# Graph layer on one core: one unit of rows in 72 fetched by SyncE instead of gathered by GpSimd

## The chip, the cores and the metric

The kernel runs on one NeuronCore of a Trainium2 chip. A core has five engines that run side by side, each with its own instruction queue: TensorE (PE, matrix products; its weight loads are shown apart as PEld), VectorE (DVE), ScalarE (ACT), GpSimd (POOL) and SyncE (SP), which computes nothing and issues transfers. Transfers run on 16 DMA engines that all queues share. The metric is the device time of one execution in microseconds.

## The reference

One layer of a graph network over 50,000 nodes with 160 features each (64 scalars and 32 vectors of three) and 1,650,000 edges, which come sorted by target node `dst`. Each edge also has four numbers `e0, e1[3]`. Cut to what matters:

```python
ss, vv = s[src], v[src]                       # the rows of x, fetched by edge
dot  = einsum('eui,ei->eu', vv, e1)
out0 = C0 * (ss * e0 @ W1 + dot * INV3 @ W2)
p3 = (ss @ W3)[:, :, None] * e1[:, None, :] * INV3
p4 = einsum('eui,uw->ewi', vv * e0[:, :, None], W4) * INV3
p5 = einsum('eui,uw->ewi', cross(vv, e1), W5) * INV6
m  = concatenate([out0, C1 * (p3 + p4 + p5)])
m_agg = segment_sum(m, dst, num_segments=n)   # sum over the edges of a node
h  = m_agg times Ws and Wv                    # linear per node
y  = x + (x + relu(h));  return layernorm(y)
```

Everything is linear in the row `x[src]` and in the edge's four numbers. So it is enough to sum, per target node, the four products of an edge number with the 160 values of the source row, and to apply one combined weight of 4 x 160 by 160 afterwards.

## The kernel before

**Units, groups, pairs.** A *unit* is 128 edges, one per partition. Six units (`G`) make a *group*, whose targets lie within 32 consecutive nodes (`W`); two groups (`PG`) make a *pair*; 20 groups (`SG`) are loaded together. There are 2087 groups, 1044 pairs and 12,522 units. The main loop `for p, (s, g, ng) in enumerate(pairs)` does, for each pair:

- `gather` (L314 to L322): one indirect DMA per unit on GpSimd (L319) that fetches 128 rows of `x`, 640 bytes each, into one slot of the tile `xg`. That tile has four buffers, so GpSimd can be up to four pairs ahead.
- `spread` (L324 to L334): VectorE makes `hot` (which of the 32 nodes each edge belongs to, L328) and `ha` (`hot` times the four edge numbers, L331).
- `group_sums` (L336 to L350): TensorE multiplies `ha` with the rows (L343), six units accumulate into one PSUM tile `ps`, and VectorE transposes it into `sums` (L349). The first matmul of a pair waits until the gathers of the whole pair have landed.
- `fetch(p)`: described below; with `HELP` empty it does nothing.

Every two pairs the weights are applied to four groups (`phc`, L579), and every block of 128 nodes is put together from these (`phb`, L639), normalised (`norm1` to `norm3`, the last writing `o` at L199) and sent out (`out<-o`, L735).

**Self edges.** Each node's edge to itself is not gathered. For the part of the list behind the first 100 groups, `pack` removes these edges from the rows of the list on VectorE and stores the shortened rows to DRAM one partition at a time (`edges<-prow`, `selves<-mine`, both L563, with the addresses loaded into registers at L546). `load` (L254) reads them back as `r`. The self edges' part is computed from `xt` and `sa` (L592, L596) in `own` (L615 to L629).

**Order.** SyncE's instructions run in the order in which the program writes them (`tc.manual_schedule(engines={ET.SP})`): in each pair a load if it is due, then `fetch(p)`, the stores of `pack`, `xt` and `sa` of a block seven pairs ahead, and the sends of finished blocks, each written eight pairs after the block's last group. The other engines' instructions are ordered by a planner when the program is built. All gathers stand in order on GpSimd, which has little else to do.

**The helper that is built in.** `HELP` names engines and periods. Where it is filled, the code before the main loop picks one unit in so many and a pair `q` that uses it, always the last unit of that pair, and divides its 128 rows into batches, spread over the pairs before (L646 to L661):

```python
nbatch = P // ROWS[eng]                     # ROWS = {ET.SP: 32, ET.Activation: 16}
at = [int(first + i * period / nbatch) // (PG * G) for i in range(nbatch)]
q = at[-1] + 2
```

`fetch(p)` (L665 to L678) then issues batch `i` at pair `p`: it loads 32 addresses into registers and starts 32 transfers of one row each:

```python
_, at = nc.values_load_multi_w_load_instructions(
    offsets[s][u:u + 1, i * nr:(i + 1) * nr], engines=[eng], ...)
for j, v in enumerate(at):
    r = i * nr + j
    queues[eng].dma_start(xr[r:r + 1, :].bitcast(U8),
                          xbytes[ds(v, 4 * D)].rearrange("(o f) -> o f", o=1))
```

The addresses come from `cast` (L265 to L276), which, when `HELP` is not empty, multiplies the source indices of each load by 640 on ScalarE into `offsets[s]`. The tile `xr` has three buffers.

Of the kernel before, what the change touches and what calls it, by code (L numbers as in the profile page):

```python
# [45 lines left out]
ET = mybir.EngineType  # L46
# [20 lines left out]
PG = 2  # L67
SG = 20

HELP = {}  # L70
HEAD = 100
RP = 128
RS = 16
# [30 lines left out]
def tile_gnn_resnorm(ctx: ExitStack, tc: tile.TileContext, x, src, dst, attr, W1, W2, W3, W4, W5, Ws, Wv, out, n_edges):  # L104
# [120 lines left out]
    with tc.tile_pool(name="once", bufs=1) as once, tc.tile_pool(name="raw", bufs=2) as rawp, \  # L225
# [18 lines left out]
        offsets = {}  # L244
        evict = nc.vector.tensor_copy if ET.Activation in HELP else nc.scalar.copy

# [18 lines left out]
        def cast(loaded):  # L265
            s, n, ri, sf, df, af = loaded
            if ri is not None:
                rf = rawp.tile([P, 2, P], F32, name="rf")
                begun.append(nc.scalar.copy(rf[:n], ri[:n]))
                sf, df = rf[:n, 0, :], rf[:n, 1, :]  # L270
            if HELP:

# [374 lines left out]
        batches, helped = {}, {}  # L647
        for h, (eng, period) in enumerate(HELP.items()):
            first = PG * G + h * period // 2
# [359 lines left out]
```

## Time and profile before

| | |
|---|---|
| median of the timed runs | 15705.15 us (15704.62 to 15706.36, 3 runs) |
| the profiled execution | 15737.51 us, span of its instructions 15735.7 us |
| GpSimd busy | 11891.8 us, 76% |
| TensorE matmuls busy | 8152.5 us, 52% |
| VectorE busy | 6035.6 us, 38% |
| ScalarE busy | 499.5 us, 3% |
| bytes moved | 1215.93 MB, 77 GB/s on average |

Times in the profile are in us unless marked ns. "Busy" leaves out register, branch, semaphore and DMA-issuing instructions, so SyncE has no busy row; its instructions are seen in the timeline as SPq. In a line of the costliest groups stand the code line, engine, operation, written tile and read tiles, shapes, count, then the busy time, the mean of one in ns, the idle time before them, and what ended that idle time. "issue" means that the engine waited for nothing that the profile shows. A line of the waits reads: who waited, for whom, the total, how often, the longest.

### The profile page before, as it was taken

Reading aid. Unit: us, or ns where it says so; the run is one execution under the profiler, and the core shown is the slowest. Engines: PE = TensorE matmul, PEld = TensorE weight load, DVE = VectorE, ACT = ScalarE, POOL = GpSimd, SP = SyncE. Lnnn points to the kernel's source line nnn. Section 1 sums busy time; section 2 is a strip of 40 time slices with the busy share of each in tenths; the row PEclk is TensorE's granted clock in tenths of the full one; section 3 lists DMA queues with packets and bytes.
Section 4 is the critical chain, followed back from the end, with each engine's and each line's share of the span. In section 5 each row is a group of like instructions: output and inputs, shape, how many; then the busy total and the mean of one; then the engine's idle time right before and its main releaser. Section 6 shows DMA issues by size and latency. Waiting matters only on the chain. (4 is left out here: it accounts for less than half of the span.)

```text
span 15735.7 us, 122013 instructions
## 1 busy us (share of the span) xinstructions
PE 8152.5 (52%) x38505; PEld 7452.0 (47%) x38506; DVE 6035.6 (38%) x11070; ACT 499.5 (3%) x1392; POOL 11891.8 (76%) x12536
## 2 busy tenths in 40 slices
PE   4554545555455555555455554554545555455555
PEld 4444545444454444444444444454444444444444
DVE  5342524325253342533425343352433425234222
ACT  0000000000000000000000000000000000000000
POOL 7777777777777777777777777777777777777777
PEclk7777777777777777777777776777777777777777
DMA  3323333233233323333233332332333332332232
GB/s 79 84 74 84 75 76 80 74 82 75 76 80 77 80 75 76 80 78 79 73 79 78 77 81 74 83 75 75 80 76 81 75 82 73 76 79 73 73 75 68
DMA packets 806901, 1215.93 MB, mean 77 GB/s; under 512 B 280851, under 2 KB 585160, under 8 KB 802278
## 3 DMA queue, kind: packets, MB, share of 16 engines
q0 software_dynamic: 601056, 1026.60, 26.6%
q1 hardware_dynamic: 203770, 180.19, 3.9%
q8 instruction: 323, 5.29, 0.1%
q14 instruction: 312, 2.56, 0.1%
q10 hardware_dynamic: 1440, 1.29, 0.0%
HBM read 1135.77 MB, written 71.40 MB: 77 GB/s over the span
## 5 line engine op out<-in xcount | busy, mean ns | idle before, releaser
L319 POOL DMA_INDIRECT xg<-in_x,si x12522 | 11887.6, 949 | 3825.5 <-issue 3777.2
L343 PE MATMUL ps<-xg,ha 128*128 128x160 f32 x25044 | 5686.4, 408 | 7298.0 <-DMA xg<-in_x,si 5676.0
L343 PEld LDWEIGHTS ps<-xg,ha 128*128 128x128 f32 x25044 | 5451.3, 281 | 7580.6 <-issue 6593.5
L349 DVE STREAM_TRANSPOSE sums<-ps 128x320 f32<-128x320 f32 x1044 | 530.7, 512 | 6311.9 <-PE ps L343 6240.0
L331 DVE TENSOR_TENSOR ha<-hot,pk 128x1536 f32<-128x1536 f32 x1044 | 1802.6, 1730 | 206.3 <-PE ps L343 206.3
L627 DVE TENSOR_SCALAR t<-yx,sa 128x160 f32<-128x160 f32 x391 | 147.5, 377 | 2585.8 <-PE yx L623 2585.5
L623 PE MATMUL yx<-BWh,xT 80*128 80x320 f32 x3128 | 1032.0, 472 | 156.6 <-ACT xT L617 152.7
L579 PE MATMUL phc<-BWk,sums 128*128 128x160 f32 x5220 | 820.6, 305 | 22.2 <-DVE t L629 19.7
L623 PEld LDWEIGHTS yx<-BWh,xT 80*128 80x128 f32 x3128 | 599.3, 202 | 439.2 <-ACT xT L617 237.4
L579 PEld LDWEIGHTS phc<-BWk,sums 128*128 128x128 f32 x5220 | 750.7, 193 | 49.6 <-issue 40.3
L639 PE MATMUL phb<-hp,hot 128*128 128x160 f32 x3474 | 562.0, 307 | 6.1 <-DVE t L629 4.3
L328 DVE TENSOR_TENSOR hot<-bank,rel 128x384 f32<-128x384 f32 x1044 | 551.1, 540 | 0.1
L639 PEld LDWEIGHTS phb<-hp,hot 128*128 128x128 f32 x3474 | 503.1, 194 | 60.5 <-issue 50.4
L629 DVE SCALAR_TENSOR_TENSOR t<-yx,sa,t 128x160 f32<-128x160 f32 x1173 | 442.6, 377 | 82.4 <-PE yx L623 67.8
L511 DVE COPY_PREDICATED prow<-marks,prow 128x2370 f32<-128x2370 int32 (+8 forms) x160 | 442.5, 2765 | 0.0
L617 ACT COPY xT<-ptx 80x256 f32<-80x256 f32 x391 | 143.8, 368 | 8133.7 <-PE ptx L615 8133.3
L581 ACT COPY hp<-phc 128x160 f32<-128x160 f32 x522 | 150.3, 288 | 5316.5 <-PE phc L579 5284.5
L511 DVE COPY_PREDICATED pra<-marks,pra 128x1580 f32<-128x1580 int32 (+8 forms) x160 | 304.5, 1903 | 0.0
L605 DVE TENSOR_TENSOR hot<-bank,rr 128x512 f32<-128x512 f32 (+2 forms) x391 | 285.3, 730 | 0.0
L640 DVE TENSOR_TENSOR phb<-phb,t 128x160 f32<-128x160 f32 x391 | 127.4, 326 | 136.1 <-PE phb L639 134.4
L615 PE MATMUL ptx<-ident,xt 128*80 128x128 f32 (+1 forms) x782 | 154.5, 278 | 38.4 <-ACT hp L581 34.1
L193 ACT ACTIVATE rstd<-mv,eps_t 128x1 f32<-128x1 f32 x391 | 115.2, 295 | 1707.3 <-DVE mv L188 1630.5
(144 smaller groups left out, 2600.6 us busy)
## 6 DMA issues: line engine op xcount, KB each, us to landing
xg<-in_x,si POOLq DMA_INDIRECT x12522
edges<-prow SPq DMA_DIRECT2D x1994, 18.5 KB
r<-edges SPq DMA_DIRECT2D x99, 360.0 KB
selves<-mine SPq DMA_DIRECT2D x1992, 0.5 KB
xt<-in_x SPq DMA_DIRECT2D x390, 80.0 KB
out<-o SPq DMA_DIRECT2D x390, 80.0 KB
pra<-in_attr SPq DMA_DIRECT2D x15, 1580.0 KB
sa<-selves SPq DMA_DIRECT2D x390, 2.0 KB
```

The source lines that it names most:

```text
L319: got.append(nc.gpsimd.indirect_dma_start(out=xg[:, j, :], out_offset=None, in_=x, in_offset=bass.IndirectOffsetOnAxis(ap=placed[0][:, u + ...
L328: nc.vector.tensor_tensor(hot[:, :n], slotsP[:, 0:W].unsqueeze(1).to_broadcast([P, n, W]), rel[:, u:u + n].unsqueeze(2).to_broadcast([P, n ...
L331: nc.vector.tensor_tensor(ha[:, :n], hot[:, :n].unsqueeze(2).to_broadcast([P, n, NK, W]), pk[:, :, u:u + n].rearrange("p k u -> p u k").un ...
L343: mm = nc.tensor.matmul(ps[:, j // G, :], ha[:, j].rearrange("p k w -> p (k w)"), xr, start=j % G == 0, stop=j % G == G - 1)
L349: nc.vector.transpose(at[:, :, i:i + ng, :].rearrange("p b g w -> p g b w"), ps[:, :ng].rearrange("p g (b f) -> p g b f", f=FB))
L511: nc.vector.copy_predicated(what[:n, a:e], mi[:, r].unsqueeze(2).to_broadcast([n, e - a, what.shape[2]]), what[:n, a + d:e + d])
L579: nc.tensor.matmul(ph[:ng * W], at[:, b, :ng].rearrange("p g w -> p (g w)"), BWk[:, b, :], start=b == 0, stop=b == ND - 1)
L605: nc.vector.tensor_tensor(hot2[:, :len(cs)], slotsP.unsqueeze(1).to_broadcast([P, len(cs), P]), rr[:, :len(cs)].unsqueeze(2).to_broadcast( ...
L615: nc.tensor.transpose(pt[:, i, :nb], xt[:nb, i * H:(i + 1) * H], ident[:nb, :nb])
L623: nc.tensor.matmul(y[:nb], xT[:, i, :nb], BWh[:, i, ks, :], start=i == 0, stop=i == 1)
L629: nc.vector.scalar_tensor_tensor(t[:nb], y[:nb, i], sa[:nb, k:k + 1], t[:nb], op0=ALU.mult, op1=ALU.add)
L639: nc.tensor.matmul(ph[:nb], hot2[:r, i, :nb], hp[:r], start=i == 0, stop=i == len(cs) - 1)
```

## The change

One constant is filled. SyncE becomes a helper with a period of 72 units.

```diff
-HELP = {}
+HELP = {ET.SP: 72}
```

With it, one unit in 72 is left out of the gathers (`n - len(others)` in `gather`), its rows come from `xr`, `fetch` issues the batches on SyncE, and `cast` makes the addresses on ScalarE. Each batch holds 32 rows, so a unit has four, and its pair is the second one after the pair of its last batch. Nothing else in the source differs; the planner orders the other engines anew.

## Prediction

> **What bounds the kernel now.** I read the page's busy shares first, then the costliest groups, then the timeline of an ordinary stretch, and last the queue of SyncE.
>
> ```profile
> span 15735.7 us, 122013 instructions
> PE 8152.5 (52%) x38505; PEld 7452.0 (47%) x38506; DVE 6035.6 (38%) x11070; ACT 499.5 (3%) x1392; POOL 11891.8 (76%) x12536
> L319 POOL DMA_INDIRECT xg<-in_x,si x12522 | 11887.6, 949 | 3825.5 <-issue 3777.2
> L343 PE MATMUL ps<-xg,ha 128*128 128x160 f32 x25044 | 5686.4, 408 | 7298.0 <-DMA xg<-in_x,si 5676.0
> q0 software_dynamic: 601056, 1026.60, 26.6%
> ```
>
> GpSimd looks 76% busy, but nearly all its idle time is "issue": it waits for nothing and is simply between two gathers. Busy plus idle is 11887.6 + 3825.5 = 15713.1 us, over 12522 gathers 1.2548 us each. That is the whole span except 9.8 us before the first gather and 18.7 us after the last. TensorE's largest idle share, 5676.0 us, is waiting for gathered rows. The DMA engines are far from full: the gather queue takes 26.6% of them.
>
> The timeline, columns start, duration, engine, line, operation, shows the pace, and what SyncE does beside it:
>
> ```profile
> 5063.20 0.30 SPq L563 DMA_DIRECT2D edges<-prow  x1
> 5063.60 0.27 SPq L563 DMA_DIRECT2D selves<-mine  x1
> 5063.96 0.23 SPq L563 DMA_DIRECT2D edges<-prow  x1
> 5064.29 0.23 SPq L563 DMA_DIRECT2D selves<-mine  x1
> 5064.61 0.23 SPq L563 DMA_DIRECT2D edges<-prow  x1
> ...
> 5189.08 0.48 DVE L199 TENSOR_SCALAR o<-y,mv,rstd 128x160 f32<-128x160 f32 x1
> 5189.59 0.37 SPq L735 DMA_DIRECT2D out<-o  x1
> 5189.81 0.95 POOL L319 DMA_INDIRECT xg<-in_x,si  x1 [0.30 <-issue]
> 5190.01 0.42 SPq L254 DMA_DIRECT2D r<-edges  x1
> 5191.06 0.95 POOL L319 DMA_INDIRECT xg<-in_x,si  x1 [0.30 <-issue]
> 5192.31 0.95 POOL L319 DMA_INDIRECT xg<-in_x,si  x1 [0.31 <-issue]
> ...
> 5197.88 6.17 PE L343 MATMUL ps<-xg,ha 128*128 128x160 f32 x24 [10.51 <-DMA xg<-in_x,si]
> ```
>
> Two things are to be seen. GpSimd keeps 1.25 us a gather while SyncE issues one-row transfers: the pace does not yield to SyncE's traffic. And SyncE's one-row transfers, with the register move before each, start 0.32 us apart. The matmul group shown is that of pair 343 (12 gathers, 24 matmuls a pair), ready 2 to 3 us after its last gather, and done within about 6 us of the pair's 12 x 1.2548 = 15.06.
>
> SyncE's own waits and the register loads (duration is least/median/most):
>
> ```profile
> SPq L735 <- DVE o L199: 10633.5, 284, 133.6
> SPq L563 <- DMA edges<-prow: 161.8, 360, 1.2
> L546 SPq TENSOR_LOAD <-spots x272: 1143/1206/1472, 293.5 to 14869.2; - x136
> L563 SPq DMA_DIRECT2D selves<-mine x2117: 227/228/1027, 364.8 to 14873.9; - x193
> ```
>
> SyncE is idle two thirds of the span, nearly all of it held at the send of a finished block until VectorE has made `o`.
>
> **The change part by part.**
>
> *Removed from GpSimd.* The helper starts at unit 12 and takes one unit every 72, as long as the pair that uses it is before pair 1044: 173 units (pairs 7, 13, 19, ... 1039). 173 x 1.2548 = **217 us** off the queue that sets the end. Against the profiled execution: 15735.7 - 217 = 15519. That execution is 0.2% above the median of the timed runs; the same 217 us there gives 15705 - 217 = 15488.
>
> [...]
>
> *Added to SyncE's queue.* Each unit is 128 rows in 4 batches of 32. A batch is a load of 32 addresses into registers, nearest row L546 with 1.206 us for 16 addresses, so 2.41 us, and 32 times a move and a one-row DMA, nearest row `selves<-mine` (one partition, 512 B, dynamic address), 0.322 us apart, so 10.3 us: 12.7 us. In all 173 x 4 x 12.7 = 8.8 ms on an engine that now uses 4236 one-row stores x 0.41 (mean spacing in their bursts, small waits included) + 272 x 1.206 + 391 blocks x 1.33 for three transfers + about 80 for the loads = 2.66 ms, or 15.3 us for every 72 units. The period for 72 units becomes 71 x 1.2548 = 89.1 us; SyncE needs 4 x 12.7 + 15.3 = 66.1 of it, 74%. It fits.
>
> The spacing of a row fetch itself is not in the trace: it reads HBM and writes SBUF, where the stores do the reverse. Bounds: below, 0.32, since the sequencer's part is the same; above, the stores' mean of 0.41, stretched because each SyncE transfer waits for the one eight before it (the 360 short waits shown) and the 18.5 KB `edges` rows hold one DMA engine for 0.71 us each. A fetched row has 640 B, and the packets of `xt<-in_x`, also HBM to SBUF, are all in within about 1 to 1.5 us of issue, under 8 x 0.32 = 2.6. I take 0.32; at 0.41 SyncE needs 77.4 of 89.1 us, which still fits.
>
> [...]
>
> *The wait that is added.* The last unit's two matmuls of a helped pair wait for SyncE's rows, and everything behind them on TensorE with them. The batches stand in SyncE's written order six, five, three and two pairs ahead, and SyncE is often held at a send. Worst place seen: the send of pair 339, shown above, is released at 5189.6, 47 us after that pair's matmuls. Behind it stand two batches for pair 343, so its rows would be in at about 5189.6 + 2 x 12.7 + 2 for the transfers between + 1.5 = 5218.5, when TensorE wants them at about 5203: 15 us late. What covers that: four row buffers. Gathers may run 4 pairs = 60.2 us from the start of one pair to the reuse of its buffer, of which 15.1 gather, 2 to 3 land and 6 are matmuls: 36 to 37 us in which TensorE may be late before GpSimd notices. TensorE needs some 10 us a pair and catches up within a few pairs. With the cover gone a late unit would cost its lateness less 36 us. If all four batches stood behind one release, 51 us plus other transfers less the 30 us of two pairs' lead is still inside it. Cost taken: 0 to 5 us in all.
>
> *Queued behind SyncE's new work*: `xt`, `sa`, `r`, the stores and `out`. `xt` is used three pairs (45 us) after it is issued and `r` four; two batches make them 25 us later. Hidden, by the same 36 us if not.
>
> *ACT* gets one multiply per load, 105 of about 0.3 us (rows `xT` 0.37, `hp` 0.29): 31 us on an engine 3% busy. It waits for the load that SyncE issues; behind it on ACT are `xT`, `hp` and `rstd`, and TensorE waits for those, again under the 36 us. *DMA engines*: the bytes are the same; 22144 packets near the 32 ns of other 640 B packets are 0.7 ms of one engine's 15.7. Nothing. [...]
>
> Sum: -217 + 0 to 5, so **15490 us**.
>
> **Rivals.** "Level" means within 0.2%, 31 us, about what a measurement of this kernel can tell.
>
> 1. *Part of the gain is stalled away* (10%). Rows come at 0.41 us; some 20 of the 391 sends are released 40 us or more after their own pair's matmuls, and if each makes GpSimd wait 5 us, 100 us go: 15590. For it: those waits. Against it: the cover of 36 us.
> 2. *SyncE becomes the bound* (16%): slower. [...]
> 3. *The change does not do what it says* (4%): the 1.25 us is the pace at which descriptors are drained, not made, and fewer gathers do not end sooner: 15705. Against it: the pace is the same with SyncE's bursts and without.
>
> **How the numbers follow.** Main case 70%, its own range 15475 to 15530. Faster is main plus rival 1, 80%; same 4%; slower 16%. The range drops rival 2 and the last of the others: below, 15460 (a little more than the 217, should the helped pairs also save the odd wait); above, 15690, the stalled case at twice its price.
>
> **What would show it.** 12349 gathers at an unchanged 1.25 us; "issue" still ending nearly all of GpSimd's idle time; 22144 `xr<-in_x` transfers on SyncE 0.32 us apart with loads of about 2.4 us a batch; SyncE's wait for `o` down from 10.6 ms to about 2; TensorE waiting for `xr` at some of the 173 places by up to 20 us. Wrong would be: rows 0.5 us apart, or GpSimd gathers whose idle time ends on a matmul `ps`.

## The result and the profile after

The changed kernel takes **15675.67 us** (median of 16 runs, 15672.77 to 15682.35) against 15705.94 us; the ratio is 0.9981, with a 95% interval of 0.9974 to 0.9988. It is faster by 30 us: the whole interval lies below 1, but the gain is still within the 31 us that the prediction calls level. A gain of 217 us was forecast. The time lies inside the stated range, but the gain is a seventh of what the reasoning promised, and the question of this section is where the other 187 us went.

The page of the changed kernel, the lines that answer to those of before:

```profile
span 15671.9 us, 167279 instructions
PE 8017.6 (51%) x38505; PEld 7282.8 (46%) x38506; DVE 6239.3 (40%) x11070; ACT 536.9 (3%) x1497; POOL 11694.9 (75%) x12363
L319 POOL DMA_INDIRECT xg<-in_x,si x12349 | 11690.7, 947 | 3931.0 <-issue 3711.2
L343 PE MATMUL ps<-xg,ha 128*128 128x160 f32 x24698 | 5320.9, 393 | 6189.6 <-DMA xg<-in_x,si 5282.4
```

GpSimd did lose its 173 gathers (12349 left). But its idle time rose, from 3825.5 to 3931.0 us, though 173 gaps of 0.30 us fell away. The waits say on what (who waited, for whom, the total, how often, the longest):

```profile
PE phc L579 <- DVE sums L349: 677.7, 173, 35.2
POOL xg L319 <- PE ps L343: 165.5, 25, 23.2
SPq L735 <- DVE o L199: 2977.8, 146, 63.0
SPq L671 <- ACT ro L274: 594.4, 32, 71.6
```

The second line was 1.5 us before: GpSimd now waits for a matmul of `ps`, that is for a free row buffer. The first is new, and its count is the number of fetched units. SyncE has used up most of its wait for `o` (10633.5 us before), as forecast. The last line is new as well: SyncE waits for the addresses that ScalarE makes.

Going through the starts of all gathers, 14 of the 16 packs have a place, once in about 60 to 70 pairs, where GpSimd stands still for 3 to 23 us. Everything over the normal spacing adds up to 175 us, against 20 us in the kernel before: **155 us of stalls**. The other loss is at the end. From the start of the last gather to the end of the span it is 46.3 us, against 18.7: **28 us**. Together 183 of the missing 187 us. (Outside the stalls the gathers of this profiled execution are 1.2503 us apart, those of the one shown for before 1.2527. Over 12,500 gathers that is 30 us, which is why the profiled executions lie 64 us apart and the medians only 30.)

One such place in the timeline, lines picked out (start, duration, engine, line, operation, and in brackets the idle time before and who ended it), with TensorE's and VectorE's work between:

```profile
1767.62 4.93 PE L343 MATMUL ps<-xg,ha 128*128 128x160 f32 x22 [2.18 <-DVE sums L349]
1773.28 2.42 PE L623 MATMUL yx<-BWh,xT 80*128 80x320 f32 x8 [0.51 <-ACT xT L617]
1775.42 2.76 DVE L511 COPY_PREDICATED prow<-marks,prow 128x2370 f32<-128x2370 int32 x1
1780.61 2.73 DVE L511 COPY_PREDICATED prow<-marks,prow 128x2346 f32<-128x2346 int32 x1
1789.73 2.47 PE L639 MATMUL phb<-hp,hot 128*128 128x160 f32 x8 [14.03 <-DVE t L629]
1791.99 0.74 PE L343 MATMUL ps<-xr,ha 128*128 128x160 f32 x2
1802.88 0.51 DVE L349 STREAM_TRANSPOSE sums<-ps 128x320 f32<-128x320 f32 x1
1803.44 3.03 PE L579 MATMUL phc<-BWk,sums 128*128 128x160 f32 x10 [10.71 <-DVE sums L349]
1823.69 6.17 PE L343 MATMUL ps<-xg,ha 128*128 128x160 f32 x24 [3.43 <-DVE ha L331]
...
1830.13 0.94 POOL L319 DMA_INDIRECT xg<-in_x,si  x1 [20.74 <-PE ps L343]
```

Two things are to be seen. VectorE is deep in a pack (the shifts of `prow`, L504 to L511), one after another; TensorE waits for `t` and then for the transpose `sums`, both of which stand behind pack steps in VectorE's queue. From 1772 to 1824 no gathered row is multiplied, 51 us, and the row buffers run out. And the two matmuls of the fetched unit, `ps<-xr`, are out of place: they belong to pair 109, whose gathered units were multiplied long before, and SyncE had issued the last of these rows at 1650, 142 us earlier.

That is so at all 173 places. Counting matmuls, those of the fetched unit run a median of 142 gathered matmuls after their pair's own, which is six pairs or 90 us. Their rows were issued some 93 us earlier, so the rows are not what they wait for. TensorE's order has changed, and VectorE's with it: the ten `prow` shift rounds of a pack took 118 us from first to last in the kernel before (median of 16) and take 49 us here. In the kernel before a pair's matmuls come between one round and the next (lines picked out):

```profile
1796.24 2.87 DVE L511 COPY_PREDICATED prow<-marks,prow 128x2370 f32<-128x2370 int32 x1
1798.74 5.91 PE L343 MATMUL ps<-xg,ha 128*128 128x160 f32 x24 [7.20 <-DMA xg<-in_x,si]
1808.01 2.86 DVE L511 COPY_PREDICATED prow<-marks,prow 128x2364 f32<-128x2364 int32 x1
```

The source asks for neither change of order; the planner made both orders anew for the program with SyncE's transfers in it.

The end, lines picked out, where the last fetched unit (pair 1039) is multiplied 20 us after the last gather began, with its blocks queued behind it:

```profile
15625.62 0.95 POOL L319 DMA_INDIRECT xg<-in_x,si  x1 [0.30 <-issue]
15645.47 0.43 PE L343 MATMUL ps<-xr,ha 128*128 128x160 f32 x2
15648.75 4.66 PE L579 MATMUL phc<-BWk,sums 128*128 128x160 f32 x20 [2.84 <-DVE sums L349]
15659.99 0.36 DVE L199 TENSOR_SCALAR o<-y,mv,rstd 80x160 f32<-80x160 f32 x1
```

### The profile page after: what moved, and what is told of

It is laid out like the page before. It is cut to its first block, busy times and chain, and to the rows that moved or that the text cites. A ratio compares the mean times of both kernels' runs of the same rounds, so it can differ in the third digit from the quotient of the medians.

```text
span 15671.9 us, 167279 instructions
## 1 busy us (share of the span) xinstructions
PE 8017.6 (51%) x38505; PEld 7282.8 (46%) x38506; DVE 6239.3 (40%) x11070; ACT 536.9 (3%) x1497; POOL 11694.9 (75%) x12363
## 5 line engine op out<-in xcount | busy, mean ns | idle before, releaser
L319 POOL DMA_INDIRECT xg<-in_x,si x12349 | 11690.7, 947 | 3931.0 <-issue 3711.2
L343 PE MATMUL ps<-xg,ha 128*128 128x160 f32 x24698 | 5320.9, 393 | 6189.6 <-DMA xg<-in_x,si 5282.4
L343 PEld LDWEIGHTS ps<-xg,ha 128*128 128x128 f32 x24698 | 5085.6, 268 | 6411.6 <-issue 5473.8
L579 PE MATMUL phc<-BWk,sums 128*128 128x160 f32 x5220 | 919.7, 329 | 784.0 <-DVE sums L349 677.7
L579 PEld LDWEIGHTS phc<-BWk,sums 128*128 128x128 f32 x5220 | 822.6, 210 | 859.5 <-DVE sums L349 720.6
L639 PE MATMUL phb<-hp,hot 128*128 128x160 f32 x3474 | 607.6, 324 | 301.4 <-DVE t L629 300.6
L639 PEld LDWEIGHTS phb<-hp,hot 128*128 128x128 f32 x3474 | 539.7, 207 | 397.8 <-issue 391.0
L511 DVE COPY_PREDICATED prow<-marks,prow 128x2370 f32<-128x2370 int32 (+8 forms) x160 | 443.4, 2771 | 0.6
L511 DVE COPY_PREDICATED pra<-marks,pra 128x1580 f32<-128x1580 int32 (+8 forms) x160 | 304.9, 1905 | 0.0
```

Source lines behind the costliest of these rows:

```text
L319: got.append(nc.gpsimd.indirect_dma_start(out=xg[:, j, :], out_offset=None, in_=x, in_offset=bass.IndirectOffsetOnAxis(ap=placed[0][:, u + ...
L343: mm = nc.tensor.matmul(ps[:, j // G, :], ha[:, j].rearrange("p k w -> p (k w)"), xr, start=j % G == 0, stop=j % G == G - 1)
L511: nc.vector.copy_predicated(what[:n, a:e], mi[:, r].unsqueeze(2).to_broadcast([n, e - a, what.shape[2]]), what[:n, a + d:e + d])
L579: nc.tensor.matmul(ph[:ng * W], at[:, b, :ng].rearrange("p g w -> p (g w)"), BWk[:, b, :], start=b == 0, stop=b == ND - 1)
L639: nc.tensor.matmul(ph[:nb], hot2[:r, i, :nb], hp[:r], start=i == 0, stop=i == len(cs) - 1)
```

## The experiments

Each run below was forecast by rival theories. Theory A at the start: the late matmuls of the fetched units cost it, because they hold one of two `ps` buffers for six pairs. Theory B: SyncE's transfers, by coming late or by disturbing others.

### The matmuls put back in their place

```diff
     for j, xr in enumerate(rows):
-        mm = nc.tensor.matmul(ps[:, j // G, :], ...)
+        with ExitStack() as behind:
+            for before in last_mm:             # last matmul of the pair before
+                behind.enter_context(tc.issue_after(before))
+            mm = nc.tensor.matmul(ps[:, j // G, :], ...)
```

`tc.issue_after(x)` binds nothing but the order: what stands in its block is issued after `x` on the engine that both share.

> The change, with one rule for the planner added: a pair's matmuls are issued behind those of the pair before it, so the fetched unit's two matmuls stand with their own pair on TensorE and not six pairs later. Theory A (the planner's late place for these matmuls, with one of the two ps buffers held meanwhile, costs 160 us of stalls and 28 us at the end): the stalls of GpSimd at the 16 packs and the long end go, 15490 to 15510 us. Theory B (the rows come too late or SyncE is overloaded, whatever the order): TensorE now waits for the rows in place, GpSimd stalls more often, 15675 us or more.

Measured: 15699.37 us, ratio 0.9995 (0.9986 to 1.0005). Theory A fails as it stands: the long end did go (26.5 us), but what lies over the normal spacing of the gathers grew from 175 to 223 us, and the ten `prow` rounds still stand within 59 us. Theory B's number came out, but not by its mechanism, since the long waits of this run are for VectorE again (the edit moves the lines behind it down by three or four):

```profile
PE phb L643 <- DVE t L633: 762.7, 57, 46.8
PE ps L346 <- DVE sums L353: 503.9, 24, 44.0
POOL xg L319 <- PE ps L346: 214.4, 28, 19.5
```

TensorE waits for VectorE, up to 47 us at once; its waits for `xr` come to 2 us in all.

### The units left out

```diff
-    return [xg[:, j, :] for j in range(n - len(others))] + others, got
+    return [xg[:, j, :] for j in range(n - len(others))] + [xg[:, 0, :] for _ in others], got
...
-            fetch(p)
```

ScalarE's multiplies for the addresses are left out too.

> The 173 units are left out of the gathers and nothing is fetched in their place; their matmuls take the rows of another unit of the pair. This is the ceiling of the change: 173 x 1.2548 us = 217 us off, 15488 us, by theories A and B. If the gather pace were that of draining the descriptors, so that fewer gathers don't end sooner: 15705 us.

Measured: 15494.68 us, ratio 0.9866 (0.9849 to 0.9882): 211 us off. The first term of the prediction stands, and the rival that gathers are drained and not made at 1.25 us falls. The `prow` rounds take 117 us here, as before: without the fetching the planner spreads them.

### The rows fetched and not used

```diff
-    for j in range(n - len(others)):
+    for j in range(n):
         got.append(nc.gpsimd.indirect_dma_start(...))
-    return [xg[:, j, :] for j in range(n - len(others))] + others, got
+    return [xg[:, j, :] for j in range(n)], got
```

> SyncE fetches all 22144 rows and ScalarE makes the addresses, but GpSimd still gathers every unit and nobody reads the fetched rows. Theory A: the fetching itself costs nothing, within 15 us of 15705 us. Theory B (the transfers disturb the gathers, or SyncE's queue delays the rest): 100 us or more above it, 15800 us.

Measured: 16149.14 us, ratio 1.0282 (1.0265 to 1.0299), 443 us slower. Taken alone this looks like Theory B at its strongest: nobody waits for the rows, and still they cost. GpSimd's waits in this run:

```profile
POOL xg L319 <- issue: 3771.3, 12374, 0.3
POOL xg L319 <- PE ps L343: 427.2, 21, 39.0
```

But the pace between stalls is unchanged (1.2503 us), the stalls are again one in a pack, 10 to 39 us each, and the `prow` rounds stand within 46 us. So there was a third candidate, which became Theory C: the new order of VectorE alone.

### One ps buffer in place of two, nothing fetched

```diff
-tc.tile_pool(name="psA", bufs=2, space=PSUM)
+tc.tile_pool(name="psA", bufs=1, space=PSUM)
```

> The kernel before, with one ps buffer in place of two, no fetching. Theory A, in which a held ps buffer makes TensorE and VectorE take turns and GpSimd stall where VectorE works on a pack: stalls of some 10 us once in a pack as in the changed kernel, 130 to 190 us slower than before, 15835 to 15895 us. If the held buffer doesn't matter: 15705 us.

Measured: 15706.56 us, ratio 1.000 (0.999 to 1.001). In VectorE's old order one `ps` buffer is enough. Whether a held buffer costs anything beside a block of pack work is not shown by this run; the next one bears on it.

### The steps of pack put behind their pairs

```diff
-            nc.vector.transpose(at[...], ps[...])
+            last_tr[:] = [nc.vector.transpose(at[...], ps[...]).ins]
...
                     if step:
-                        step()
+                        with ExitStack() as behind:
+                            for tr in last_tr:
+                                behind.enter_context(tc.issue_after(tr))
+                            step()
```

A pack step may now not be issued on VectorE before the transpose of the pair in which the program writes it.

> The change, with each step of pack put behind VectorE's transpose of the pair in which the program writes it, so that the planner can't gather these steps into one block ahead of the pairs' own work. Theory C (the planner, with SyncE's 22144 transfers in its reckoning, orders VectorE anew and packs the shift steps of a pack into 46 to 59 us instead of 118 us; TensorE then stands still for 60 to 80 us, more than the four row buffers cover): the stalls at the packs go, 15510 to 15540 us, the longer end and the late matmuls of the fetched units still there. Theory B (SyncE is too slow in the stage where it also stores): still 15650 us or more.

Measured: 15519.88 us, ratio 0.9881 (0.9864 to 0.9897). The same fetching, 156 us faster than the changed kernel. What is over the normal spacing of the gathers is 24 us, from 175, and the end is still 46.4 us long. GpSimd's waits in this run:

```profile
POOL xg L319 <- issue: 3725.3, 12222, 0.3
POOL xg L319 <- DMA xg<-in_x,si: 13.9, 35, 1.1
...
POOL xg L319 <- PE ps L343: 5.9, 9, 2.4
```

The wait for `ps` is gone, and nothing came in its place. The `prow` rounds take 114 us again, and TensorE's longest gap between gathered matmuls at a pack is 14 to 48 us, against 37 to 69 in the changed kernel and 11 to 15 in the kernel before. The matmuls of the fetched units are as late here as in the changed kernel (142 matmuls), so the buffers that they hold do not make the stalls by themselves. What they leave is the long end.

### Both rules together

> The same, and the matmuls of a pair behind those of the pair before it. Theory C: 15490 to 15515 us, nearly the ceiling of 15495. Theory B: TensorE waits in place for rows that come late, 15650 us or more.

Measured: 15493.19 us, ratio 0.9864 (0.9847 to 0.9880). The end is 26.8 us long. This is the ceiling of the run with the units left out (15494.68), and what was forecast for the change. The group of the gathers of this run, then the fetches, the fetched units' matmuls and what TensorE waited for before these:

```profile
L319 POOL DMA_INDIRECT xg<-in_x,si x12349 | 11689.8, 947 | 3773.8 <-issue 3724.6
```

```profile
L680 SPq DMA_DIRECT2D xr<-in_x x22144: 227/228/1772, 7.8 to 15350.2; - x200
L346 PE MATMUL ps<-xr,ha x346: 297/299/606, 161.5 to 15436.2; 128*128 128x160 f32 x173
...
  DMA xr<-in_x: 7.9, 4
```

The last line is the answer to Theory B at this period: with the matmuls in place TensorE waits for fetched rows 4 times, 7.9 us in all.

### The rule alone, nothing fetched

The edit is that of the pack steps, on the kernel before.

> The kernel before with the steps of pack behind the pair's transpose, nothing fetched. By every theory within 15 us of 15706: the order there spreads these steps already.

Measured: 15706.30 us, ratio 1.000 (0.999 to 1.0009). The rule is worth nothing by itself; it only keeps an order that the kernel before had anyway.

### Fetched, not used, and paced

> All rows fetched and none used, every unit gathered, as in the run unread, with pack's steps behind the pairs' transposes. Theory C (unread lost its 443 us to VectorE's order alone, the 22144 transfers cost nothing): 15700 to 15725 us. Theory B (the transfers themselves cost): 15800 us or more, up to the 16149 of unread.

Measured: 15757.61 us, ratio 1.0032 (1.0019 to 1.0044). Of the 443 us of the run without the rule 392 are gone, so that loss was the order. The rest is 51 us, more than expected: one stall of 27 us at pair 20 and an end of 39.6 us in place of 18.7 us, both seen in the trace, make 48 of it. What ordered these two differently was not tried. Between pair 20 and the end the longest stall is 5.1 us, where the kernel before has one of 4.8, with 22144 transfers running beside the gathers.

### A block of pack work, nothing fetched

```diff
-    steps += [partial(next, g, None)] * n_                # the shift rounds of prow
+    steps += [partial(block_of, g)] + [None] * (n_ - 1)   # all in one step
...
-    has[p + 1] = spread(...)
+    with tc.issue_after(last shift):                      # where there is one
+        has[p + 1] = spread(...)
```

> The kernel before, with nothing fetched, but the 10 rounds that shift prow of a pack written as one step and the next pair's spread put behind them, so that VectorE runs some 53 us of pack work in one block as it does in the changed kernel. Theory C (the block alone makes the loss): GpSimd stalls about 10 to 20 us at each of the 16 packs, 15860 to 16020 us. Theory B (the loss needs SyncE's row transfers): 15706 us.

Measured: 15758.57 us, ratio 1.0033 (1.0021 to 1.0046). Neither theory's number came out: 52 us are lost, one stall of 45 us at the first pack and less than 3 us at each of the others (the last has the 4.6 us that the kernel before has there too). The reason is in the gaps. In this run TensorE goes 46.5 to 48.3 us from one gathered matmul to the next at each later pack, and 92 us at the first. In the changed kernel most of the stalling packs have 50 to 69 us, in the run with the rows not used 57 to 87. Set beside each other the three runs give one rule where TensorE was on time going in: a gap of 48 us costs 0 to 2, 56 costs 7 to 8, 69 costs 22 to 23, 79 costs 33, 92 costs 45. Of the 14 stalling packs of the changed kernel seven go by it. Six went in late, with matmuls that started 16 to 20 us after their pair's last gather where 3 us is usual, so that gaps of 37 to 51 us cost 3 to 20 (one is the timeline shown); the last has two long gaps in a row. So the block alone fills the cover to its edge and no further. What takes the changed kernel over it is, as far as these traces tell, the block together with TensorE's new order beside it, the waits of 14 us for `t` and 11 us for `sums` in the timeline above. Why the gap at the first pack of this run is 92 us was not looked into. The share of each in one stall was not tried apart; binding the pack steps removed them all, binding the matmuls alone did not.

### How far it goes

With both rules, a shorter period; only the number 72 differs.

> Both rules for the planner and one unit in 60 fetched, some 207 units: the ceiling is 15706 - 207 x 1.25 = 15447. Theory C: 15450 to 15480, since SyncE needs 4 x 12.7 + 12.8 = 63.6 us of the 74 us of a period. Theory B: slower than with one in 72, since where SyncE also stores it needs more than the period.

Measured: 15448.53 us, ratio 0.9836 (0.9819 to 0.9852), with 208 units fetched, for which the ceiling is 15446. This is the fastest of all kernels run here.

> Both rules for the planner, one unit in 54, some 231 units: ceiling 15706 - 231 x 1.25 = 15417. SyncE needs 50.8 us of a period of 66.5 for the rows and 11.5 on average for the rest, but where it also stores it is asked for some 4 us a pair more, a little over the whole: if the 36 us of cover carry that stage, 15420 to 15440; if not, stalls there and 15450 to 15550.

Measured: 15455.67 us, ratio 0.9840 (0.9823 to 0.9856), the second of the two cases. Two stalls in the first 750 us, 27 us together, and an end of 32 us take back what 23 further units saved. The two stalls are Theory B's, in the first stage with stores: TensorE waited 37 us for `xr` at the first, and at the second 16 us for `xt` and 15 us for `r`, which SyncE issues too. After that the cover carried the stages with stores.

> Both rules, one unit in 48, some 260 units: ceiling 15381. SyncE needs 50.8 + 10.2 = 61 us on average of a period of 59, so SyncE is the bound: about 260 x 61 us and more, 15850 us or above.

Measured: 16316.79 us, ratio 1.0390 (1.0372 to 1.0407). Here SyncE is the bound, and the waits show it:

```profile
PE ps L346 <- DMA xr<-in_x: 4448.3, 228, 53.3
POOL xg L319 <- PE ps L346: 959.9, 117, 27.2
```

TensorE now does wait for `xr`, 228 times, and SyncE's own wait for `o` is down to 27 us. The excess over the ceiling of 15381, 936 us over 260 units, is 3.6 us on a period of 59. So an estimate from the measured time is that SyncE needs about 62 us for one unit and the rest of its work, where 61 had been reckoned.

## Why the prediction was right or wrong

**What bounds the kernel: right.** The gathers are made at 1.25 us each; leaving 173 out saved 211 us of the forecast 217. 173 × 1.250 us is 216 us, and the end after the last gather is 24.5 us in that run against 19.1 us in the kernel before with its pack steps held (the traced execution at the same pace), which makes 211.

**SyncE's cost: right.** Rows start 0.323 us apart (0.322 taken), 10.5 us a batch (10.3 taken), and a load of 32 addresses takes 2.16 us (2.41 taken). The instruction that fetches a row takes 228 ns, as that of `selves<-mine` did in the kernel before, so the nearest row was the one to take. Rows 0.5 us apart, which the prediction names as a sign of being wrong, are not the pace of the changed kernel: the mean within a batch is 0.335 us. A fetched row's packet ended 0.95 us after its issue at the median, and within 1.33 us for 99 in 100 (the 272 batches of the changed kernel with no other 640-byte packets of that queue beside them), which is under the 2.6 us reckoned. (`xt<-in_x` in the kernel before is not quite as fast as read: in 83 transfers that can be told apart 120 of the 128 packets were in 1.7 us after the issue at the median, the last at 2.7 us.) That a second engine issues cost the gathers nothing that could be measured: with both orders bound the change gained 213 of the 216 us that 173 gathers take at 1.250 us, and the run that fetches nothing in their place gained 211.

**The added wait: the step that failed.** "Cost taken: 0 to 5 us in all" was reckoned for rows that come late to matmuls in their old place. The matmuls were not in their old place, and where they stood the rows had been issued some 93 us before. The term was 183 us: 155 of stalls at the packs and 28 at the end. What it was reckoned for is small: with both orders bound, and the matmuls in place, TensorE waited 7.9 us for rows in all. (There the last row of a unit is issued 54 us before the last of its pair's gathered matmuls, at the median. In the changed kernel it is 10 us, and at 79 of the 173 places less than 2 us or after it: where the matmuls run late, so does SyncE.) The step that failed is that the old trace's order of VectorE and TensorE was carried over. "The change" says that the planner orders the other engines anew, and the prediction passed over it. The working priced every queue that the change writes to and left the queues that the planner writes, those of VectorE and TensorE, as the old trace showed them. Once VectorE's pack steps were held where the program writes them, 156 us came back; once TensorE's matmuls were held too, the other 27. Why the planner gathers the pack steps when SyncE fetches is not known; the run with the rows fetched and not used shows only that the fetching and its address multiplies, with none of the rows on TensorE, are enough for it.

**The cover of 36 us: about right in size, wrong in use.** A gap of 48 us between gathered matmuls, 33 over the usual 15, was just free, and beyond it each microsecond cost about one. But it was held against one lateness of 15 us at a time, and pack blocks of 50 us were not looked for, because the old order had none.

**The sums for SyncE.** The reckoned 66 of 89 us at one unit in 72, and 64 of 74 at one in 60, both left room, and both kernels reached their ceiling with the orders bound. At 54 and 48 the bound appeared about where the sum over all of SyncE's work put it.

**Rivals.** The first (part of the gain stalled away) came true in its effect, and more than it allowed, not by its cause. That the time still lies inside the range is luck: the upper end was drawn for rows that come late. The second was refuted at 72, began at 54 and was met at 48. The third fell with the run that left the units out. The signs listed to look for were the right ones: GpSimd's idle time ending on `ps` was named as what would make the forecast wrong, and that is what the page showed.

## What to carry to other kernels

Where a planner orders the instructions, a change on one engine's queue is a change on all: before a gain is forecast, ask which of the other queues have long work that nothing in the source holds to its place (here the packs). When a gain goes missing, look not at the new work but at what stands in front of the old: here the new instructions were early, and the loss was between two old ones. A run that does the added work without using it can mislead in the same way, since it is ordered anew too; it told the causes apart only once the order was bound.

## What was not expected of the hardware

The gathers were seen at two paces: outside the stalls 1.2527 us in the profiled execution of before, 1.2501 to 1.2506 in those of all other kernels here, 0.2% for the whole span. The profiled execution of before took 15737.5 us and its timed runs 15704 to 15707, which fits two paces of one and the same kernel; the cause is not known. A sum made against one execution carries that.

SyncE's 22144 one-row transfers of 640 bytes moved that pace by no more than 0.0003 us (1.2504 us with them, both rules bound, and 1.2501 with the units left out).
